# Low-rank product over all 128 rows, adapter products one token tile later, first query chunk two tiles later, in a fused mixing and attention kernel

## The chip, the cores and the metric

The kernel runs on one core of a Trainium2 chip. The metric is the device time of one execution in microseconds (us). Three runs of the kernel before gave 1172.77, 1173.44 and 1174.05 us; the median, 1173.44, is the time before.

The engines are named as in the profile: PE (TensorE, with PEld for its weight loads), DVE (VectorE), ACT (ScalarE), POOL (GpSimd) and SP (SyncE, which here mostly issues DMAs). A matrix product takes its stationary operand through a weight load and streams the other operand's columns. Products land in PSUM, which has eight banks of 2 KB a partition; everything else stands in SBUF, 128 partitions wide.

## The reference

`x` is 32 batches x 32 tokens x 512 features, float32 like everything here. Four layers are added one after the other:

```python
# L0: mix the 32 tokens of a batch with one of 16 small matrices (32 x 32)
x = x + einsum('bct,bcd->bdt', x, weights[condition])
# L1: one base matrix for all, and a low-rank addition with a picked A
low = einsum('bsi,bir->bsr', x, lora_A[labeler_index])        # rank 32, 5 labelers
x = x + einsum('bsi,oi->bso', x, W) + 0.5 * einsum('bsr,or->bso', low, lora_B)
# L2: one of 8 matrices (512 x 512) for each batch
x = x + einsum('bsi,boi->bso', x, weight[adapter_ids])
# L3: attention: 32 query and 8 key heads of 128, rmsnorm and rope on q and k,
#     512 cached keys in 16 pages and 32 new ones a batch, output product Wo
x = x + attention(x, Wq, Wk, Wv, Wo, k_cache, v_cache, ...)
```

## The kernel before

**Tiles and parts.** The 1024 tokens are cut into eight token tiles of 128 (four batches each, `NT` = 8, `BT` = 4), the 512 features into four chunks of 128 (`KC` = 4). The query, key and value matrices form twelve chunks of 512 columns: eight of queries, two of keys, two of values. The program has a first part (L0, L1, L2 and the first query chunk, tile by tile; lines 423 to 667), a second part that projects the other chunks, and a third with the attention. The first ends about 135 us into the span. The change edits only the first part; no instruction of the other two is added or removed.

**One tile's way through the first part.** Each step names its line in the kernel before.

- `gather_mix` (L443): an indirect DMA from GpSimd fetches the mixing matrices `mg` of the tile's four batches.
- `mixers` (L457): VectorE spreads them into a block-diagonal 128 x 128 matrix `md` and adds the identity, so that the product gives x + L0.
- `mix` (L471): four products of 128 columns give the transposed result in PSUM; ScalarE copies it to `x1t` (L475).
- `low_1` (L490): four products with `la`, the A matrices of all five labelers side by side (160 columns). VectorE masks the four that aren't wanted (the pick, L494) and sums what is left to `low`, 128 tokens x 32 (L501).
- `base` (L504 to 516): TensorE transposes `low` (L508, 32 rows come out), ScalarE scales it by 0.5 into `lowt` (L510), four products with the base matrix `wb` fill a PSUM bank (L513), and one product over 32 rows, `lowt` with `lb` (the B matrix), is added to it (L514; the profile counts each float32 product twice, so a "pair"). VectorE copies the bank to `xs` (L516). The sum x + L0 isn't added to it separately: VectorE adds the identity to `wb` once, in four steps (L636).
- `flip_2` (L480, L481): four transposes and ScalarE's copy give `x2t`.
- `adapt` (L533): sixteen products with four batch-picked adapter matrices `wa`, each over a column group of 32; VectorE adds the result to `xs` (L540).
- `transposed(..., "x3t")` (again L480, L481): the transposed input of the projections.
- `projected(c, t, lag)` (L308 to 384): a chunk's four products, then squares on ScalarE (L335), their sums, roots and reciprocals, the rotation on VectorE and GpSimd (L351, L356, L362), four scalings on ScalarE (L366), a transpose on VectorE into `st`, and four DMAs of it to `q_d` from SP (L384). The last two come `lag` projections later than their own.

**What sets the order.** In the loop of the first part, PE's and DVE's instructions stay in the order in which the program writes them (`manual_schedule`). ACT, POOL and SP are placed by a scheduler; `issue_after` keeps an instruction behind another in that placement. Before the loop the order is mix 0, mix 1, low 0, low 1, mix 2, the identity into `wb`, base 0, low 2, flip_2 0, base 1, adapt 0, then `constants` and `angles` (the rotation tables). A round n then takes mix n, base n-1, flip_2 n-2, low n, x3t of tile n-3, adapt n-2, and from n = 4 on the first query chunk of tile n-4. From n = 8 on, where mix and low have run out, that query projection stands ahead of x3t instead of behind the adapter products.

**Buffers.** Eight PSUM banks are in three pools: `ps_tr` (two banks: x1t, low, lowt, x2t, x3t), `ps_m` (four) and `ps_n` (two); `accumulator` takes every third bank from `ps_n` and the others from `ps_m`. `wa` has eight buffers of 1 MB, two tiles' worth, so that the loads for tile t+2 are issued after `adapt(t)` (`adapt_and_load`). `st` has three.

**Loads.** They are all issued by SP, in this order: `la`, held behind the first `mg` by a tiny ScalarE copy into `la` that has to come first (the gate, L581); `wb`, `lb`, the fourth tile of x, the adapter matrices of tile 0, the rotary table `fr`, the norm weights, more of x, the adapter matrices of tile 1, the first query chunk's weights `wq` 0 between tiles 5 and 6 of x, and then the adapter matrices tile by tile with the stores of `st` among them. `wq` 1 stands after round 4's adapter loads.

The functions that the diff touches, and what calls them, with the profile's line numbers:

Of the kernel before, what the change touches and what calls it, by code (L numbers as in the profile page):

```python
# [12 lines left out]
F32 = mybir.dt.float32  # L13
I32 = mybir.dt.int32
AF = mybir.ActivationFunctionType
ALU = mybir.AluOpType
AX = mybir.AxisListType
# [3 lines left out]
P = 128  # L21
B, S, HID = 32, 32, 512
# [5 lines left out]
NT = B * S // P  # L28
BT = P // S
KC = HID // P  # L30
# [27 lines left out]
def cond_resid_kernel(  # L58
# [18 lines left out]
    nc = tc.nc  # L77
# [48 lines left out]
    def constants():  # L126
        with tc.issue_after(rows_known.ins):
            constant_values()
# [163 lines left out]
    def x3t(t: int):  # L292
        return x3_all[:, :, t * P : (t + 1) * P]
# [9 lines left out]
    def load_qkv(c: int, eng=nc.sync):  # L303
        ws[c] = wqps[c % 2].tile([P, KC, HID], F32, tag="wq", name=f"wq_{c}")
        eng.dma_start(out=ws[c], in_=w_qkv[c])
# [85 lines left out]
    def projected(c: int, t: int, lag: int):  # L391
        u = project(c, t)
        if u is not None:
            for stage in (squares, sums, roots, inverses, rotate, scales):
                stage(u)
            ready.append(u)
        if len(ready) > lag or (u is None and ready):
            store_heads(ready.pop(0))
# [22 lines left out]
    with ExitStack() as p1:  # L421
# [3 lines left out]

        wb = w1p.tile([P, KC, HID], F32, name="wb")
        la = w1p.tile([P, KC, NL * R], F32, name="la")
        lb = w1p.tile([R, HID], F32, name="lb")

        ones = w1p.tile([P, HID], F32, name="ones")  # L430
        nc.vector.memset(ones, 1.0)
# [5 lines left out]
        )  # L437

        mgs, x1ts, lows, x2ts, was = {}, {}, {}, {}, {}

        def gather_mix(t: int):
            mg = sp.tile([P, S], F32, tag="mg", name=f"mg_{t}", bufs=4)
# [23 lines left out]
        def mix(t: int):  # L466

            md = mds.pop(t)
            px = ps_tr.tile([P, KC, P], F32, tag="tr", name=f"x1t_ps_{t}")
            for k in range(KC):  # L470
                nc.tensor.matmul(  # L471
                    px[:, k, :], xs[:, t, k * P : (k + 1) * P], md, start=True, stop=True
                )
            x1ts[t] = sp.tile([P, KC, P], F32, tag="x1t", name=f"x1t_{t}", bufs=3)
            nc.scalar.copy(x1ts[t], px)  # L475

        def transposed(t: int, dst: bass.AP, name: str):
            pt = ps_tr.tile([P, KC, P], F32, tag="tr", name=f"{name}_ps_{t}")
            for k in range(KC):
                nc.tensor.transpose(pt[:, k, :], xs[:, t, k * P : (k + 1) * P], ident)  # L480
            nc.scalar.copy(dst, pt)  # L481
# [3 lines left out]
        which = w1p.tile([P, NT, NL], F32, name="which")  # L485

        def low_1(t: int):
            plo = ps_tr.tile([P, NL * R], F32, tag="tr", name=f"low_ps_{t}")
            for k in range(KC):
                nc.tensor.matmul(  # L490
                    plo, x1ts[t][:, k, :], la[:, k, :], start=(k == 0), stop=(k == KC - 1)
                )
            picked = sp.tile([P, NL, R], F32, tag="picked", name=f"picked_{t}", bufs=1)
            nc.vector.tensor_tensor(  # L494
                picked,
                plo.rearrange("p (l r) -> p l r", l=NL),
                which[:, t, :].unsqueeze(2).to_broadcast([P, NL, R]),
                ALU.mult,
            )
            lows[t] = sp.tile([P, R], F32, tag="low", name=f"low_{t}", bufs=3)  # L500
            nc.vector.tensor_reduce(  # L501
                lows[t], picked.rearrange("p l r -> p r l"), AX.X, ALU.add
            )

        def base(t: int):
            xt = x1ts.pop(t)
            plt = ps_tr.tile([R, P], F32, tag="tr", name=f"lowt_ps_{t}")
            nc.tensor.transpose(plt, lows.pop(t), ident)  # L508
            lowt = sp.tile([R, P], F32, tag="lowt", name=f"lowt_{t}")
            nc.scalar.mul(lowt, plt, LORA_SCALING)  # L510
            pb = accumulator(f"base_{t}")
            for k in range(KC):
                nc.tensor.matmul(pb, xt[:, k, :], wb[:, k, :], start=(k == 0), stop=False)  # L513
            nc.tensor.matmul(pb, lowt, lb, start=False, stop=True)  # L514

            nc.vector.tensor_copy(xs[:, t, :], pb)  # L516
# [61 lines left out]
        load_x(1)  # L578
        load_x(2)

        nc.scalar.copy(la[:, 0, 0:1], mgs[0][:, 0:1])  # L581
        gate = nc.sync.dma_start(out=la, in_=lora_a)
        loads = ExitStack()
        loads.enter_context(tc.issue_after(gate.ins))
        nc.sync.dma_start(out=wb, in_=w_base)
        nc.sync.dma_start(out=lb, in_=lora_b)
        load_x(3)
        for b in range(BT):
            load_adapt(b)
# [5 lines left out]
            load_adapt(b)  # L595
        with tc.issue_after(picked[-1]):
            load_x(5)
            load_qkv(0)
            load_x(6)
            load_x(7)  # L600
        with tc.issue_after(rows_known.ins):
# [4 lines left out]
        with tc.manual_schedule(engines={mybir.EngineType.PE, mybir.EngineType.DVE}):  # L606

            idle = ps_tr.tile([P, HID], F32, tag="tr", name="idle_ps")
            for n in (HID, HID, P, P, P, P, P, P):
                nc.tensor.matmul(idle[:, :n], ones[:, :P], ones[:, :n], start=True, stop=True)  # L610

            def ahead_of(t: int):
                if t + 3 < NT:
                    gather_mix(t + 3)
                if t < NT:
                    mixers(t)

            def adapt_and_load(t: int):
                adapt(t)
                if t + 2 < NT:  # L620
                    for j in range(BT):
                        load_adapt((t + 2) * BT + j)


            ahead_of(0)
            mix(0)
            ahead_of(1)
            mix(1)
            ahead_of(2)
            low_1(0)  # L630
            low_1(1)
            mix(2)

            for k in range(KC):
                d = wb[:, k, k * P : (k + 1) * P]
                nc.vector.tensor_tensor(d, d, ident, ALU.add)  # L636
            base(0)
            low_1(2)
            ahead_of(3)
            flip_2(0)  # L640
            base(1)
            adapt_and_load(0)
            constants()
            angles()
            for n in range(3, NT + 3):
                if n < NT:
                    mix(n)
                if n - 1 < NT:
                    base(n - 1)
                if n - 2 < NT:  # L650
                    flip_2(n - 2)
                if n < NT:
                    low_1(n)
                    ahead_of(n + 1)
                if n >= NT and n - 4 < NT:
                    projected(0, n - 4, 1)
                if n - 3 < NT:
                    transposed(n - 3, x3t(n - 3), "x3t")
                if n - 2 < NT:
                    adapt_and_load(n - 2)  # L660
                if 4 <= n < NT:
                    projected(0, n - 4, 1)
                if n == 4:
                    with tc.issue_after(picked[-1]):
                        load_qkv(1)
            projected(1, 0, 2)
            projected(0, NT - 1, 2)

# [430 lines left out]
```

## Time and profile before

| | kernel before |
|---|---|
| median of three runs | 1173.44 us (1172.77 to 1174.05) |
| profiled execution, its own time | 1172.88 us |
| its span, first to last instruction | 1170.9 us |
| PE busy | 1157.9 us (99%) |
| DVE busy | 797.4 us (68%) |
| ACT busy | 752.8 us (64%) |
| POOL busy | 431.4 us (37%) |
| granted TensorE clock | 1.000 |
| moved by DMA | 250.64 MB, 214 GB/s on average |
| PE's share of the chain that ended last | 92% |

The profiled execution took 2.0 us more than its span; that lies around the instructions. Rows of the timeline give the start in us from the span's start, the busy time, the engine, the line, the operation, output and inputs with their tile, the partitions and elements, and how many instructions of one kind stand together; the bracket holds the idle time of the engine ahead of them and what ended it. On PE a row's busy time overlaps the next row's, since products are pipelined: the time that one takes is the distance from its start to the next start. Rows of the stretches give for each window the span, the busy time of PE, PEld, DVE, ACT and POOL, each with its number of instructions, the granted clock, the mean busy share of the 16 DMA engines, and GB/s.

### The profile page before, as it was taken

What the parts mean: (1) busy time and instruction counts of PE and PEld (TensorE: products, weight loads), DVE (VectorE), ACT (ScalarE), POOL (GpSimd) and SP (SyncE); (2) the same over time, 40 slices, a digit from 0 to 9 for tenths busy, and PEclk for the clock granted to TensorE, in tenths of its full rate; (3) what the DMA queues carried; (4) which work ended last, traced back from release to release, by engine and by line L of the source; (5) the groups of instructions that cost most, each with busy time, mean ns of one, the idle gap of its engine ahead of it and who ended that gap; (6) DMA issues with size and microseconds to landing.
All of it is one profiled execution on the core that took longest, in us unless ns stands there. A gap on an engine that the chain in (4) does not pass through costs nothing.

```text
span 1170.9 us, 19713 instructions
## 1 busy us (share of the span) xinstructions
PE 1157.9 (99%) x5512; PEld 745.1 (64%) x5512; DVE 797.4 (68%) x1782; ACT 752.8 (64%) x1652; POOL 431.4 (37%) x567
## 2 busy tenths in 40 slices
PE   8999999999999999999999999999999999999998
PEld 5444444444444467777777777777777777777766
DVE  2433488777777157877777777777777877876861
ACT  1222366565656268877777877877877777877760
POOL 3301444333333044434433443443344344344410
PEclk9999999999999999999999999999999999999999
DMA  8997765655544646789777677767766776775710
GB/s 323 418 355 289 271 188 135 174 159 155 154 113 114 212 132 226 247 269 271 225 242 232 212 223 240 228 210 227 251 208 208 256 226 198 252 247 189 227 45 10
DMA packets 180879, 250.64 MB, mean 214 GB/s; under 512 B 21250, under 2 KB 140674, under 8 KB 175010
## 3 DMA queue, kind: packets, MB, share of 16 engines
q1 hardware_dynamic: 156802, 163.52, 44.8%
q0 software_dynamic: 19216, 69.35, 17.6%
q10 hardware_dynamic: 4752, 16.52, 4.0%
q8 instruction: 45, 0.74, 0.3%
q14 instruction: 64, 0.52, 0.2%
HBM read 219.94 MB, written 29.36 MB: 213 GB/s over the span
## 4 chain that ended last, share of the span: by engine, by line
PE 92%; DMA 2%; DVE 2%; SPq 1%; issue 1%; ACT 1%; POOL 0%; another core or an unknown queue 0%; DVEq 0%; ACTq 0%; POOLq 0%
PE qkv L308 28%; PE o_ps L818 18%; PE f_ps L895 17%; PE s_ps L747 11%; PE s_ps L748 9%; PE adapt L533 2%; PE base L513 2%; PE o_ps L838 2%; DMA wa<-in_w_adapt_dram 1%; PE pn_ps L805 1%; PE f_ps L915 1%; PE f_ps_last L915 1%; SPq L194 1%; PE base L514 1%; DMA kt<-in_k_cache_dram 0%
## 5 line engine op out<-in xcount | busy, mean ns | idle before, releaser
L790 ACT COPY placed<-turned 32x512 f32<-32x512 f32 x539 | 332.1, 616 | 33.0 <-DVE turned L778 23.7
L818 PEld LDWEIGHTS o_ps<-vt,placed 128*128 128x128 f32 x2048 | 267.3, 191 | 117.1 <-issue 95.5
L308 PE MATMUL qkv<-wq,x3t 128*128 128x512 f32 x768 | 336.9, 593 | 0.3 <-ACT vs L315 0.3
L756 DVE CUSTOM_DVE_ANT_0 pr<-s_ps,mask 128x544 f32<-128x544 f32 x256 | 185.4, 724 | 163.0 <-PE s_ps L748 150.5
L765 ACT ACTIVATE pr<-pr,low 128x544 f32<-128x544 f32 x256 | 191.6, 749 | 133.0 <-DVE low L756 91.7
L818 PE MATMUL o_ps<-vt,placed 128*128 128x128 f32 x2048 | 270.5, 275 | 2.2 <-DVE ot L875 1.3
L308 PEld LDWEIGHTS qkv<-wq,x3t 128*128 128x128 f32 x768 | 145.1, 190 | 171.4 <-issue 167.9
L792 POOL COPY placed<-turned 32x512 f32<-32x512 f32 x268 | 163.4, 610 | 230.2 <-DVE turned L778 176.4
L895 PE MATMUL f_ps<-wo,ot 128*128 128x512 f32 x480 | 241.3, 594 | 0.3
L362 POOL TENSOR_TENSOR ra<-ra,rs 128x512 f32<-128x512 f32 x80 | 101.8, 1272 | 220.9 <-DVE rs L356 196.0
L778 DVE STREAM_TRANSPOSE turned<-pr 128x512 f32<-128x512 f32 x256 | 178.6, 697 | 0.1
L747 PE MATMUL s_ps<-kt,qt 128*128 128x288 f32 x512 | 173.6, 421 | 0.6 <-issue 0.4
L748 PE MATMUL s_ps<-kt,qt 128*128 128x256 f32 x512 | 152.4, 379 | 1.5 <-DMA kt<-in_k_cache_dram 1.5
L246 POOL DMA_INDIRECT vt<-in_v_cache_dram,v_idx x128 | 127.8, 998 | 36.0 <-issue 25.0
L366 ACT ACTIVATE ra<-ra,rinv 128x128 f32<-128x128 f32 x320 | 101.8, 390 | 36.2 <-POOL ra L362 21.4
L748 PEld LDWEIGHTS s_ps<-kt,qt 128*128 128x128 f32 x512 | 97.1, 190 | 29.0 <-issue 2.3
L895 PEld LDWEIGHTS f_ps<-wo,ot 128*128 128x128 f32 x480 | 85.8, 190 | 28.2 <-issue 13.9
L794 DVE COPY placed<-turned 32x512 f32<-32x512 f32 x217 | 96.3, 444 | 5.5
L747 PEld LDWEIGHTS s_ps<-kt,qt 128*128 128x128 f32 x512 | 77.4, 191 | 13.3 <-DVE low L756 6.1
L335 ACT ACTIVATE sq<-qkv 128x512 f32<-128x512 f32 x80 | 47.3, 591 | 59.6 <-PE qkv L308 59.0
L801 POOL COPY pq<-pr 128x128 f32<-128x128 f32 x64 | 18.5, 289 | 178.0 <-ACT pr L765 162.2
L351 DVE TENSOR_TENSOR ra<-qkv,cw 128x512 f32<-128x512 f32 x80 | 54.8, 685 | 35.3 <-ACT sq L335 35.3
(97 smaller groups left out, 747.6 us busy)
## 6 DMA issues: line engine op xcount, KB each, us to landing
kt<-in_k_cache_dram SPq DMA_DIRECT2D x512, 128.0 KB
wa<-in_w_adapt_dram SPq DMA_DIRECT2D x32, 1024.0 KB
q_d<-st SPq DMA_DIRECT2D x256, 64.0 KB
qt<-q_d SPq DMA_DIRECT2D x64, 256.0 KB
wq<-in_w_qkv_dram ACTq DMA_DIRECT2D x10, 1024.0 KB
wo<-in_w_o_dram SPq DMA_DIRECT2D x16, 320.0 KB
k_d<-st SPq DMA_DIRECT2D x64, 64.0 KB
v_d<-vs ACTq DMA_DIRECT2D x16, 256.0 KB
```

Source lines behind the costliest of these rows:

```text
L246: nc.gpsimd.indirect_dma_start(out=vts[b][:, c, :], out_offset=None, in_=v_cache, in_offset=bass.IndirectOffsetOnAxis(ap=v_idx[:, at : at ...
L308: nc.tensor.matmul(ps, x3t(t)[:, k, :], ws[c][:, k, :], start=(k == 0), stop=(k == KC - 1))
L362: nc.gpsimd.tensor_tensor(u.a, u.a, s, ALU.add)
L747: nc.tensor.matmul(ps[:, first:L], q, kt4[:, :N_LOW, g, :], start=True, stop=True)
L748: nc.tensor.matmul(ps[:, L : first + LT], q, kt4[:, N_LOW:, g, :], start=True, stop=True)
L756: nc.vector.tensor_tensor_reduce(pr, ps[:, first : first + LT], mask, -SCALE, 3.0e38, ALU.add, ALU.min, low)
L765: nc.scalar.activation(pr, pr, AF.Exp, bias=low, scale=-1.0, accum_out=dens[quad][:, u : u + 1])
L778: nc.vector.transpose(part, pr)
L790: nc.scalar.copy(dst, src)
L792: nc.gpsimd.tensor_copy(dst, src)
L818: nc.tensor.matmul(po, pt[:, c, :], vt[:, c, g * D : (g + 1) * D], start=(c == 0 and q == 0), stop=(c == L // P - 1 and q == 1),)
L895: nc.tensor.matmul(pfs[t][:, :HID], ots[t, h // HALF][:, h % HALF, :], wo(h), start=(h == 0), stop=(h == (HQ if t < NT - 1 else HALF) - 1),)
```

## The change

Three things change in the first part.

The low-rank product runs over 128 rows. `lb` has 128 rows, zeroed by GpSimd and then filled in the first 32; `low` is one of three 128 x 128 tiles that were zeroed once, of which the reduction writes the first 32 columns; its transpose is 128 x 128, stands after the third of the four base products, and the product with `lb` is over all rows. The result of `low_1`'s products takes a bank of `ps_m` and not of `ps_tr`.

The rounds are shifted. Round n has adapt n-3 (was n-2), x3t of tile n-4 (was n-3) and, from n = 6 on, the first query chunk of tile n-6 (was n-4). There is one round more; two of the first chunk's tiles stand behind the loop. `constants` and `angles` follow the first adapter products in round 3.

The loads are moved. `la` goes first without a gate, and the gate is on `wb`. `wq` 0 leaves its place among the first loads for the place behind the fourth tile's adapter matrices, and `wq` 1 goes behind the sixth's. The four additions of the identity to `wb` stand ahead of the first pick on VectorE.

```diff
--- before.py
+++ after.py
@@ -425,7 +425,8 @@
 
         wb = w1p.tile([P, KC, HID], F32, name="wb")
         la = w1p.tile([P, KC, NL * R], F32, name="la")
-        lb = w1p.tile([R, HID], F32, name="lb")
+        lb = w1p.tile([P, HID], F32, name="lb")
+        nc.gpsimd.memset(lb, 0.0)
 
         ones = w1p.tile([P, HID], F32, name="ones")
         nc.vector.memset(ones, 1.0)
@@ -437,6 +438,11 @@
         )
 
         mgs, x1ts, lows, x2ts, was = {}, {}, {}, {}, {}
+
+
+        wide = [w1p.tile([P, P], F32, name=f"low_{i}") for i in range(3)]
+        for low in wide:
+            nc.gpsimd.memset(low, 0.0)
 
         def gather_mix(t: int):
             mg = sp.tile([P, S], F32, tag="mg", name=f"mg_{t}", bufs=4)
@@ -485,7 +491,7 @@
         which = w1p.tile([P, NT, NL], F32, name="which")
 
         def low_1(t: int):
-            plo = ps_tr.tile([P, NL * R], F32, tag="tr", name=f"low_ps_{t}")
+            plo = ps_m.tile([P, HID], F32, tag="mm", name=f"low_ps_{t}")[:, : NL * R]
             for k in range(KC):
                 nc.tensor.matmul(
                     plo, x1ts[t][:, k, :], la[:, k, :], start=(k == 0), stop=(k == KC - 1)
@@ -497,20 +503,21 @@
                 which[:, t, :].unsqueeze(2).to_broadcast([P, NL, R]),
                 ALU.mult,
             )
-            lows[t] = sp.tile([P, R], F32, tag="low", name=f"low_{t}", bufs=3)
+            lows[t] = wide[t % 3]
             nc.vector.tensor_reduce(
-                lows[t], picked.rearrange("p l r -> p r l"), AX.X, ALU.add
+                lows[t][:, :R], picked.rearrange("p l r -> p r l"), AX.X, ALU.add
             )
 
         def base(t: int):
             xt = x1ts.pop(t)
-            plt = ps_tr.tile([R, P], F32, tag="tr", name=f"lowt_ps_{t}")
-            nc.tensor.transpose(plt, lows.pop(t), ident)
-            lowt = sp.tile([R, P], F32, tag="lowt", name=f"lowt_{t}")
-            nc.scalar.mul(lowt, plt, LORA_SCALING)
             pb = accumulator(f"base_{t}")
             for k in range(KC):
                 nc.tensor.matmul(pb, xt[:, k, :], wb[:, k, :], start=(k == 0), stop=False)
+                if k == KC - 2:
+                    plt = ps_tr.tile([P, P], F32, tag="tr", name=f"lowt_ps_{t}")
+                    nc.tensor.transpose(plt, lows.pop(t), ident)
+                    lowt = sp.tile([P, P], F32, tag="lowt", name=f"lowt_{t}")
+                    nc.scalar.mul(lowt, plt, LORA_SCALING)
             nc.tensor.matmul(pb, lowt, lb, start=False, stop=True)
 
             nc.vector.tensor_copy(xs[:, t, :], pb)
@@ -578,12 +585,12 @@
         load_x(1)
         load_x(2)
 
-        nc.scalar.copy(la[:, 0, 0:1], mgs[0][:, 0:1])
-        gate = nc.sync.dma_start(out=la, in_=lora_a)
+        nc.sync.dma_start(out=la, in_=lora_a)
+        nc.scalar.copy(wb[:, 0, 0:1], mgs[0][:, 0:1])
+        gate = nc.sync.dma_start(out=wb, in_=w_base)
         loads = ExitStack()
         loads.enter_context(tc.issue_after(gate.ins))
-        nc.sync.dma_start(out=wb, in_=w_base)
-        nc.sync.dma_start(out=lb, in_=lora_b)
+        nc.sync.dma_start(out=lb[:R, :], in_=lora_b)
         load_x(3)
         for b in range(BT):
             load_adapt(b)
@@ -595,7 +602,6 @@
             load_adapt(b)
         with tc.issue_after(picked[-1]):
             load_x(5)
-            load_qkv(0)
             load_x(6)
             load_x(7)
         with tc.issue_after(rows_known.ins):
@@ -627,22 +633,19 @@
             ahead_of(1)
             mix(1)
             ahead_of(2)
+
+            for k in range(KC):
+                d = wb[:, k, k * P : (k + 1) * P]
+                nc.vector.tensor_tensor(d, d, ident, ALU.add)
             low_1(0)
             low_1(1)
             mix(2)
-
-            for k in range(KC):
-                d = wb[:, k, k * P : (k + 1) * P]
-                nc.vector.tensor_tensor(d, d, ident, ALU.add)
             base(0)
             low_1(2)
             ahead_of(3)
             flip_2(0)
             base(1)
-            adapt_and_load(0)
-            constants()
-            angles()
-            for n in range(3, NT + 3):
+            for n in range(3, NT + 4):
                 if n < NT:
                     mix(n)
                 if n - 1 < NT:
@@ -652,17 +655,21 @@
                 if n < NT:
                     low_1(n)
                     ahead_of(n + 1)
-                if n >= NT and n - 4 < NT:
-                    projected(0, n - 4, 1)
+                if n >= NT:
+                    projected(0, n - 6, 1)
+                if 0 <= n - 4 < NT:
+                    transposed(n - 4, x3t(n - 4), "x3t")
                 if n - 3 < NT:
-                    transposed(n - 3, x3t(n - 3), "x3t")
-                if n - 2 < NT:
-                    adapt_and_load(n - 2)
-                if 4 <= n < NT:
-                    projected(0, n - 4, 1)
-                if n == 4:
+                    adapt_and_load(n - 3)
+                if n == 3:
+                    constants()
+                    angles()
+                if 6 <= n < NT:
+                    projected(0, n - 6, 1)
+                if n in (4, 6):
                     with tc.issue_after(picked[-1]):
-                        load_qkv(1)
+                        load_qkv(n // 2 - 2)
+            projected(0, NT - 2, 1)
             projected(1, 0, 2)
             projected(0, NT - 1, 2)
 
```

## The prediction, on record before the result

> **What bounds the kernel now.** I read the page's busy times and chain first, then TensorE's timeline for the first 135 us (all edits lie there), then the other engines', SyncE's issues and the DMA rate where TensorE waits.
>
> The page:
>
> ```profile
> PE 1157.9 (99%) x5512; PEld 745.1 (64%) x5512; DVE 797.4 (68%) x1782; ACT 752.8 (64%) x1652; POOL 431.4 (37%) x567
> ...
> PE 92%; DMA 2%; DVE 2%; SPq 1%; issue 1%; ACT 1%; POOL 0%; another core or an unknown queue 0%; DVEq 0%; ACTq 0%; POOLq 0%
> ```
>
> TensorE sets the time: whatever shortens its stream in the first part moves the end one for one, since no product of the later parts changes. The start, in the timeline of all engines:
>
> ```profile
> 9.91 1.32 PE L490 MATMUL low_ps<-la,x1t 128*128 128x160 f32 x8 [0.58 <-DMA la<-in_lora_a_dram]
> 11.89 0.59 ACT L475 COPY x1t<-x1t_ps 128x512 f32<-128x512 f32 x1 [2.83 <-PE low_ps L490]
> ...
> 13.77 1.16 PE L471 MATMUL x1t_ps<-md,xs 128*128 128x128 f32 x8
> ...
> 15.32 3.70 PE L513 MATMUL base<-wb,x1t 128*128 128x512 f32 x8 [0.28 <-DVE wb L636]
> ```
>
> The second copy of x1t starts at 11.89 although its products ended at 9.33. TensorE's timeline further on:
>
> ```profile
> 49.21 1.06 PE L533 MATMUL adapt<-wa,x2t 128*32 128x512 f32 x6
> 50.77 3.62 PE L533 MATMUL adapt<-wa,x2t 128*32 128x512 f32 x26 [0.50 <-DMA wa<-in_w_adapt_dram]
> 54.32 3.70 PE L308 MATMUL qkv<-wq,x3t 128*128 128x512 f32 x8
> ...
> 63.94 1.25 PE L490 MATMUL low_ps<-la,x1t 128*128 128x160 f32 x8
> 65.79 0.66 PE L480 MATMUL x3t_ps<-ident,xs 128*128 128x128 f32 x4 [0.60 <-ACT x2t L481]
> ...
> 74.38 0.27 PE L508 MATMUL lowt_ps<-ident,low 128*32 128x128 f32 x1
> 74.49 3.60 PE L513 MATMUL base<-wb,x1t 128*128 128x512 f32 x8
> 78.02 1.12 PE L514 MATMUL base<-lb,lowt 32*128 32x512 f32 x2
> 79.07 0.66 PE L480 MATMUL x2t_ps<-ident,xs 128*128 128x128 f32 x4
> 79.56 1.25 PE L490 MATMUL low_ps<-la,x1t 128*128 128x160 f32 x8
> ```
>
> Read start to start. The third adapter product takes 54.32-49.21 = 5.11 us, the others 3.57: it waits for its weights. Low to x3t takes 1.85, elsewhere 1.09: ScalarE is late. And the 32-row pair (L514) costs more than its columns: 1.05 where a quarter of eight products' 3.44 (qkv 108.27 to 111.71) is 0.86; the base before it takes 3.53, not 3.44; the x2t behind it 0.49, not 4 x 0.11. SyncE's issues, and the DMA stretches behind the last of them:
>
> ```profile
> 84.83 3.08 SPq L158 DMA_DIRECT2D wa<-in_w_adapt_dram  x4
> 92.29 1.75 SPq L384 DMA_DIRECT2D q_d<-st  x4
> 99.63 3.06 SPq L158 DMA_DIRECT2D wa<-in_w_adapt_dram  x4
> ```
>
> ```profile
> 110.00:112.00 2.00, 2.00 (x8) 0.99 (x7) 0.00 (x0) 0.03 (x1) 0.00 (x0) 1.00 0.92 338
> 112.00:114.00 2.00, 2.00 (x22) 0.64 (x24) 1.04 (x3) 1.34 (x3) 0.00 (x0) 1.00 0.35 105
> ```
>
> Four adapter matrices issued at 99.63 have moved (4.2 MB, summed over the stretches) between 112 and 113: 12.4 to 13.5 us after the issue. Those of 84.83 take until about 97.
>
> **The change, part by part.**
>
> *Low-rank pair over 128 rows.* The products keep their number and columns; what goes is 0.19 + 0.09 + 0.05 = 0.33 to 0.34 us at each of eight tiles: 2.7 us. The transposed product now stands between the third and fourth base product; it costs 0.11 as before (74.38 to 74.49). Its copy on ScalarE has to end inside what follows it, 0.11 + 0.86 = 0.97: alone it takes 0.27 + 0.26 plus some 0.06 of signals, so it is covered; behind a copy of 0.59 it took until 32.04 from 31.04 and would cost up to 0.2 a tile. I take 0; bounds 0 and 1.6.
> The Trainium skill (TensorE: Matmul & The Clock Gate, Why this matters for your kernels) says a lone product of 32 rows takes as long as one of 128, by which widening gains nothing and the sum is 2.7 worse. The same skill (TensorEngine Tiling (Array Packing), Key Properties) says that a change of tiling mode drains TensorE. The rows agree with the second at L514, and not at L508, whose 32 columns also change the mode and cost no more than their 0.11; the rows decide.
>
> *Adapter products one tile later.* Tile 2's weights: with the earlier starts below, adapt(0) ends at about 35.4, and the weights issued then land by 49, where adapt(2) is due at 53.7. The wait goes: 1.5 us. wq(0) is issued behind the fourth tile's weights (adapt(1) ends 46.4; 13 us for them, 2.5 for 1 MB at 415 GB/s: 62) and is due at 68; wq(1) has 50 us.
> The low product has banks of another pool now, and x2t a whole round before its use: the 0.8 us at 65.79 goes. The table load (1.28) falls under base(6), before its low-rank copy.
>
> *The tail.* Between adapt(5)'s end and adapt(7) there stood 20.7 us (99.62 to 120.34). Now there stand x2t, qkv, x3t, adapt(6), qkv, x3t: 0.49 + 3.44 + 0.53 + 3.57 + 3.54 + 0.53 = 12.1. Their weights can be issued only at adapt(5)'s end, and on SyncE's queue they now stand behind the second query tile's four stores, which come 3.8 us behind their product (88.45 to 92.29), so just before adapt(5)'s end, and take 1.75: the loads start 1.6 to 1.9 later than that end. 1.7 + 12.4 to 13.5 = 14.1 to 15.2, against 12.1: a new wait of 2.0 to 3.1, up to 3.4 if the stores' small rows share the engines. I take 2.9: the run of 99.63 is the nearest.
>
> *The start.* la (0.33 MB) leaves the gate; wb goes at 6.74 and not 7.14. The identity's four adds (0.89) stand before the first pick on VectorE and wait for wb; even if it lands at 12 they and two picks (1.5) end by 14.5, and the low values are due at 17.2. base(0) follows the third mix directly: 13.77 + 0.89 = 14.66 and not 15.32, if the copy at 11.89 stays late: 0.7 gained. What made that copy late no row shows. Bounds: -0.3 (the gathers share the engines with la; the third, beside it, came about 0.9 slower than the second) and 3.0 (copy at 9.35, base(0) at 12.3). I take 0.7, what these rows show. GpSimd's four memsets (0.55 by the iota of equal width, 3 x 0.2) less the three small jobs that move behind the gathers (0.73) are 0.4, inside its 1.38 idle before the first gather.
>
> *Nothing on the path:* the angles' 7.4 us on VectorE now follow adapt(0) at 35.4; base(3)'s copy, a pick and the next mixer queue behind them and end at 45.4, mix(5) is due at 46.3. If that cover goes, mix(5) pays.
>
> **Sum:** 2.7 + 1.5 + 0.8 + 0.7 - 2.9 = 2.8. The profiled execution took 1172.88 (span 1170.9 and 2.0 around it), so 1170.1; the median shown is 0.56 above it: 1173.44 - 2.8 = **1170.6**, 0.24% less.
>
> **Rivals.**
> *The start clears.* The late copy is gone with la's wait: base(0) at 12.3, 2.3 us more: 1168.3. For it: the copy's releaser is the low product that itself waited for la. Against: low and its pick were late too (ended 11.23, picked 13.39), after la was there. 22%.
> *No wait at adapt(7)*, if the last weights come within 12 us: 1167.7. Against: three batches that took 12.4 or more. 8%.
> *The pair gains nothing*, its copy being late or the drain elsewhere (the first rule above): 1172.5 to 1173.3. Against: equal overheads in every tile's rows. 10%.
> *Slower: the stores.* Four query tiles now run without filler, not three, and in the built order 16 key pages and a 0.4 us load stand before the seventh tile's store, where 13 pages stood. VectorE waited 3.43 us for such a store at 149.9. Pages took 1.4 each, so it comes 4 us later after adapt(7), as the products do by 3.5: a bank that was read at 155.3 and needed at 162 keeps some 6.5 us. Beyond that TensorE pays each us; at 2.2 a page the store is 12 later and the time 1176. 10%.
>
> **How the numbers follow.** My forecast has 50%; its own range is 1169.8 to 1171.8 (new wait 2.0 to 3.4, start -0.3 to 1, copies up to 0.8). 0.2% (2.35 us) is what a measurement of this kernel can tell from no change: below 1171.1 is faster. Two thirds of the forecast (0.33) and the first two rivals (0.30) are faster: 0.63; the rest of it and the third rival are the same: 0.27; slower 0.10. Range 1167.8 to 1172.9: it leaves out the slower rival and the low ends.
>
> **What would show it.** L521 pair to x2t 0.86 at each tile, base with its transposed product 3.55; no wait before adapt(2) to adapt(6); a wait of 2 to 3.4 us on wa before adapt(7) at about 111; base(0) at 14.7; the first product of the second query chunk's second tile near 131.8 (134.7 before). Wrong: if L521 waits for its copy, if adapt(7) does not wait, or if qkv waits for VectorE between 135 and 175.

## The result and the profile after

Over 20 runs each the changed kernel took 1171.84 us and the kernel before 1174.36 (medians); the ratio is 0.9979, 95% interval 0.9972 to 0.9986. That is 2.5 us (1.6 to 3.3) faster, where 2.8 was forecast. The profiled execution's own time is 1172.15 us, its span 1170.3. The page still has TensorE as the bound:

```profile
PE 1155.9 (99%) x5512; PEld 745.8 (64%) x5512; DVE 798.6 (68%) x1782; ACT 753.1 (64%) x1652; POOL 430.7 (37%) x571
...
PE 91%; DMA 3%; DVE 3%; issue 1%; SPq 1%; ACT 1%; POOL 0%; another core or an unknown queue 0%; DVEq 0%; ACTq 0%; POOLq 0%
```

One round of TensorE's timeline, by which the low-rank pair is read:

```profile
72.79 2.74 PE L515 MATMUL base<-wb,x1t 128*128 128x512 f32 x6
75.37 0.27 PE L518 MATMUL lowt_ps<-ident,low 128*128 128x128 f32 x1
75.47 1.02 PE L515 MATMUL base<-wb,x1t 128*128 128x512 f32 x2
76.34 1.02 PE L521 MATMUL base<-lb,lowt 128*128 128x512 f32 x2
77.19 0.60 PE L486 MATMUL x2t_ps<-ident,xs 128*128 128x128 f32 x4
77.63 1.25 PE L496 MATMUL low_ps<-la,x1t 128*128 128x160 f32 x8
78.72 0.60 PE L486 MATMUL x3t_ps<-ident,xs 128*128 128x128 f32 x4
```

The pair now takes 0.85 (76.34 to 77.19; 1.05 before) and x2t behind it 0.44 (0.49). Base with its transposed product takes 3.55 (3.64). The pair does not wait for its copy: 0.87 after the fourth product, as its columns ask. From low to x3t it is 1.09; the 0.76 us that were lost here once are gone. The third adapter set does not wait: its 32 records stand in one row. What came instead stands at the eighth, in the same timeline:

```profile
53.76 3.64 PE L540 MATMUL adapt<-wa,x2t 128*32 128x512 f32 x32
...
110.30 0.60 PE L486 MATMUL x3t_ps<-ident,xs 128*128 128x128 f32 x4
110.83 1.61 PE L540 MATMUL adapt<-wa,x2t 128*32 128x512 f32 x6
114.29 3.62 PE L540 MATMUL adapt<-wa,x2t 128*32 128x512 f32 x26 [1.84 <-DMA wa<-in_w_adapt_dram]
117.84 3.70 PE L308 MATMUL qkv<-wq,x3t 128*128 128x512 f32 x8
```

117.84 - 110.83 less the usual 3.57 is a wait of 3.44 us. SyncE's queue shows why the weights come then:

```profile
98.64 1.76 SPq L384 DMA_DIRECT2D q_d<-st  x4
100.98 3.06 SPq L158 DMA_DIRECT2D wa<-in_w_adapt_dram  x4
```

The sixth adapter set ended at 98.74. The loads that it releases are issued at 100.98, behind the second query tile's stores, and the last products start 13.3 us after that. A second new wait is 0.44 us ahead of the sixth mix: the second adapter set starts at 42.32, so the mix was due at 45.89.

```profile
46.33 1.13 PE L477 MATMUL x1t_ps<-md,xs 128*128 128x128 f32 x8 [0.38 <-issue]
```

The start, in the timeline of all engines:

```profile
2.90 0.43 SPq L588 DMA_DIRECT2D la<-in_lora_a_dram  x1
...
7.91 0.29 DVE L463 TENSOR_TENSOR md<-mg,quarter 128x128 f32<-128x128 f32 x1 [4.10 <-DMA mg<-in_w_mix_dram,c_idx]
...
8.58 2.05 PE L477 MATMUL x1t_ps<-md,xs 128*128 128x128 f32 x16 [1.58 <-DVE md L463]
...
11.18 0.59 ACT L481 COPY x1t<-x1t_ps 128x512 f32<-128x512 f32 x1 [0.81 <-PE x1t_ps L477]
13.01 1.05 PE L477 MATMUL x1t_ps<-md,xs 128*128 128x128 f32 x8
13.59 0.90 DVE L639 TENSOR_TENSOR wb<-wb,ident 128x128 f32<-128x128 f32 x4 [4.01 <-DMA wb<-in_w_base_dram]
13.94 2.84 PE L515 MATMUL base<-wb,x1t 128*128 128x512 f32 x6
```

The first mixer comes at 7.91 (6.60 before), the first mix at 8.58 (7.38 before); yet the first base product starts at 13.94 and not at 15.32. The second copy of x1t, at 11.89 before, is at 11.18 here. The additions to wb wait until 13.59 for wb to land (the prediction allowed for 12), and the first base product follows the first of them by 0.35; it does so in five of the ten profiled runs of the new order, so wb's landing is close to being the next limit there.

At the second query chunk's second tile TensorE is 2.56 us ahead (121.81 + 3 x 3.44 = 132.1 against 134.7). The rows account for 2.46 of it: pair 8 x 0.333 = 2.66, third adapter set 1.54, x2t 0.76, start 1.38, less the two new waits of 3.44 and 0.44.

### The profile page after: what moved, and what is told of

Same layout as the page of the kernel before. It is cut to its first block, busy times and chain, and to the rows that moved or that the text cites. A ratio compares the mean times of both kernels' runs of the same rounds, so it can differ in the third digit from the quotient of the medians.

```text
span 1170.3 us, 19720 instructions
## 1 busy us (share of the span) xinstructions
PE 1155.9 (99%) x5512; PEld 745.8 (64%) x5512; DVE 798.6 (68%) x1782; ACT 753.1 (64%) x1652; POOL 430.7 (37%) x571
## 4 chain that ended last, share of the span: by engine, by line
PE 91%; DMA 3%; DVE 3%; issue 1%; SPq 1%; ACT 1%; POOL 0%; another core or an unknown queue 0%; DVEq 0%; ACTq 0%; POOLq 0%
PE qkv L308 28%; PE o_ps L825 18%; PE f_ps L902 16%; PE s_ps L754 11%; PE s_ps L755 9%; PE base L515 2%; PE adapt L540 2%; PE o_ps L845 2%; DMA kt<-in_k_cache_dram 1%; DMA wa<-in_w_adapt_dram 1%; PE x1t_ps L477 1%; PE pn_ps L812 1%; PE low_ps L496 1%; PE f_ps L922 1%; PE f_ps_last L922 1%
## 6 DMA issues: line engine op xcount, KB each, us to landing
kt<-in_k_cache_dram SPq DMA_DIRECT2D x512, 128.0 KB
```

## The experiments

The kernel before ran beside each group on the same chip. Where an interval stands, it is that of the ratio to it. "Second chunk" is the start of TensorE's product of the second query chunk's second tile, from which on all kernels have the same products; the last column is the span less that. Each row's times are of one profiled run.

| kernel | first mix | first base | wait at the eighth adapter set | second chunk | the rest |
|---|---|---|---|---|---|
| before | 7.38 | 15.32 | 0 | 134.7 | 1036.2 |
| changed | 8.58 | 13.94 | 3.44 | 132.1 | 1038.2 |
| changed, profiled again | 8.17 | 13.24 | 2.59 | 130.6 | 1037.7 |
| pair alone | 7.51 | 13.11 | 0 | 133.3 | 1036.2 |
| narrow pair in the new order | 8.60 | 13.60 | 2.67 | 133.4 | 1035.5 |
| query tile before the last adapter set | 8.14 | 13.25 | 0 | 128.0 | 1035.9 |
| stores behind loads | 7.75 | 12.93 | 0.44 | 128.1 | 1036.9 |
| la gated again | 7.49 | 13.35 | 2.61 | 130.6 | 1037.2 |
| x's third tile behind the gate | 7.50 | 14.02 | 2.74 | 131.4 | 1036.4 |
| pair in halves (order of before) | 7.43 | 15.35 | 0 | 134.9 | 1035.3 |
| mixers before tables | 7.84 | 13.25 | 2.56 | 130.0 | 1037.0 |
| query tile and mixers | 7.79 | 13.21 | 0 | 127.4 | 1037.2 |
| stores and mixers | 7.84 | 13.21 | 0.62 | 128.1 | 1037.6 |

### The pair alone

```diff
 # in the kernel before: lb, low and lowt over 128 rows, zeroed as in the change;
 # the transposed product stays ahead of the base products
-        lb = w1p.tile([R, HID], F32, name="lb")
+        lb = w1p.tile([P, HID], F32, name="lb")
+        nc.gpsimd.memset(lb, 0.0)
...
-            lows[t] = sp.tile([P, R], F32, tag="low", name=f"low_{t}", bufs=3)
+            lows[t] = wide[t % 3]
...
-            plt = ps_tr.tile([R, P], F32, tag="tr", name=f"lowt_ps_{t}")
+            plt = ps_tr.tile([P, P], F32, tag="tr", name=f"lowt_ps_{t}")
```

> Only the low-rank pair over 128 rows, in the order of before (the transposed product still ahead of the base products). My theory (the 32-row pair costs 0.19 + 0.09 + 0.05 us a tile beyond its columns): pair to x2t 0.86 instead of 1.05, x2t 0.44 instead of 0.49, the first tile of the second query chunk's rows 2.6 us earlier than before (132.1 for the second tile, before 134.69), the time 2.5 to 2.8 us under the kernel before. Rival (a lone product takes as long over 32 rows as over 128, and the gain came from the new order): the pair's rows unchanged, the time as before within 0.3 us.

1172.33 us against 1173.62, ratio 0.9992 (0.9984 to 1.0001). Its timeline:

```profile
46.84 2.10 PE L537 MATMUL adapt<-wa,x2t 128*32 128x512 f32 x6
50.38 3.62 PE L537 MATMUL adapt<-wa,x2t 128*32 128x512 f32 x26 [1.44 <-DMA wa<-in_w_adapt_dram]
53.94 3.70 PE L308 MATMUL qkv<-wq,x3t 128*128 128x512 f32 x8
...
65.40 0.66 PE L484 MATMUL x3t_ps<-ident,xs 128*128 128x128 f32 x4 [0.95 <-ACT x2t L485]
...
77.53 1.02 PE L518 MATMUL base<-lb,lowt 128*128 128x512 f32 x2
78.39 0.60 PE L484 MATMUL x2t_ps<-ident,xs 128*128 128x128 f32 x4
78.83 1.25 PE L494 MATMUL low_ps<-la,x1t 128*128 128x160 f32 x8
```

The rows are as the theory has them: 0.86 and 0.44 in the old order too, so the rival falls. The time is not: 2.5 to 2.8 us were expected, the ratio gives 0.9 (-0.1 to 1.9), and TensorE is 1.4 ahead at the second chunk. The third adapter set was due at 46.84 instead of 49.21 and went on at 50.38 instead of 50.77, since its weights came at about the same time. All but 0.4 us of what was gained ahead of it, the start's 2.2 us included, went into that wait, which grew from 1.54 to 3.53; another 0.35 went into the wait ahead of x3t (63.20 to 65.40 is 2.20 from low to x3t, 1.85 before). Why the weights came no earlier: from 10 us to 52 the DMA engines' share is 0.98 to 1.03 in every stretch of this run, so they were full. One of the stretches, share of the engines and GB/s last:

```profile
40.00:45.00 5.00, 5.00 (x18) 2.56 (x18) 0.20 (x2) 0.77 (x2) 5.00 (x5) 1.00 1.03 426
```

So in the old order about half of the pair's 2.7 us (four of the eight tiles stand ahead of that wait) did not reach the end; the shift takes the wait out of the way.

### The narrow pair in the new order

```diff
 # in the changed kernel: lb, low and lowt over 32 rows again
-        lb = w1p.tile([P, HID], F32, name="lb")
-        nc.gpsimd.memset(lb, 0.0)
+        lb = w1p.tile([R, HID], F32, name="lb")
...
-                    plt = ps_tr.tile([P, P], F32, tag="tr", name=f"lowt_ps_{t}")
+                    plt = ps_tr.tile([R, P], F32, tag="tr", name=f"lowt_ps_{t}")
```

> The whole change but with the pair over 32 rows again (transposed product still behind the third base product). My theory: 0.33 us a tile come back, 2.6 in all, less what the wait at the eighth tile's adapter products gives up when TensorE comes later to it: the products up to the sixth adapter set come 6 x 0.33 = 2.0 later and so do the loads that they release, and only the 0.33 between that point and the wait are hidden by it. So 2.3 us slower than the changed kernel, about equal to before (within 0.6 us). Rival: the pair's width is worth nothing and the time stays with the changed kernel, 2.5 under before.

1171.46 us, ratio 0.9989 (0.9979 to 0.9998): 1.3 us under before, where about none was expected. In the trace:

```profile
76.75 0.27 PE L513 MATMUL lowt_ps<-ident,low 128*32 128x128 f32 x1
76.86 1.02 PE L510 MATMUL base<-wb,x1t 128*128 128x512 f32 x2
77.81 1.12 PE L516 MATMUL base<-lb,lowt 32*128 32x512 f32 x2
78.86 0.66 PE L481 MATMUL x2t_ps<-ident,xs 128*128 128x128 f32 x4
79.36 1.25 PE L491 MATMUL low_ps<-la,x1t 128*128 128x160 f32 x8
```

All three parts of the price are back: 0.95 for the product ahead of the pair (0.87 wide), 1.05 for the pair, 0.50 for x2t. Against the changed kernel as profiled again, the second chunk starts 2.9 us later, of which 0.4 is the start; against its first profile 1.3, above all because the wait at the eighth adapter set was 0.8 longer there. By the rows the width is worth 0.33 us a tile in this order too. In the time less can be told: 1.3 us (0.2 to 2.5) under before with the narrow pair, 2.5 (1.6 to 3.3) with the wide one, and the two intervals overlap. The expectation, equal to before within 0.6, missed: it was reckoned from the changed kernel's first profile, whose wait was 0.8 longer than this run's.

### The pair in halves

```diff
-            nc.tensor.matmul(pb, lowt, lb, start=False, stop=True)
+            for h in (0, 1):
+                c = slice(h * HID // 2, (h + 1) * HID // 2)
+                nc.tensor.matmul(pb[:, c], lowt, lb[:, c], start=False, stop=(h == 1))
```

> The kernel before with the 32-row product cut in two halves of 256 columns, still over 32 rows: same columns, one change into and one out of the 32-row form, twice the instructions. If the extra 0.33 us a tile is paid at the change of form: from its first product to x2t still 1.05 to 1.10 us, base before it 3.53, x2t behind it 0.49. If each product over 32 rows pays: 1.25 us or more from its first product to x2t.

```profile
74.73 3.60 PE L513 MATMUL base<-wb,x1t 128*128 128x512 f32 x8
78.26 1.13 PE L516 MATMUL base<-lb,lowt 32*128 32x256 f32 x4
79.31 0.66 PE L480 MATMUL x2t_ps<-ident,xs 128*128 128x128 f32 x4
79.81 1.25 PE L490 MATMUL low_ps<-la,x1t 128*128 128x160 f32 x8
```

One run: 1172.21 us (1173.97 for the kernel before). Twice the instructions over 32 rows, and still 1.05 us from the first to x2t, 3.53 ahead and 0.50 behind. The 0.33 us belong to going into the 32-row form and out of it, not to a product. The Trainium skill (TensorEngine Tiling (Array Packing), Key Properties) says that a change of tiling mode drains TensorE; this trace agrees in so far as the change of rows has a price, 0.33 us for the way in and out; that it is a drain no row shows. There is no such price for the transposed product over 32 columns, which takes 0.11 like the one over 128. The adapter products, though, which have 128 rows and column groups of 32, have longer neighbours in the changed kernel: x3t ahead of them takes 0.53 (110.30 to 110.83) and 0.43 ahead of a query product (121.38 to 121.81), x2t behind them 0.49 (98.74 to 99.23) and 0.44 behind the wide pair. No run here gives them another form, so whether that is the same price is not shown.

### One more query tile ahead of the last adapter set

```diff
-                if n >= NT:
+                if NT <= n < NT + 3:
                     projected(0, n - 6, 1)
+                if n >= NT + 2:
+                    projected(0, n - 5, 1)
...
-            projected(0, NT - 2, 1)
             projected(1, 0, 2)
```

> The change with one more tile of the first query chunk moved ahead of the eighth tile's adapter products (the sixth query tile, whose input is there), and the seventh moved up in the same way; nothing else. My theory: the 3.44 us wait for the last adapter matrices is a matter of the work between the sixth and eighth adapter sets; 3.44 us more work there fills it. Wait 0 to 0.3 us, the second query chunk's second tile at 128.7 to 129.0 (132.1 in the changed kernel), the time 3.1 to 3.5 under the changed kernel and 5.6 to 6.0 under before. Rival: VectorE and the stores cannot follow the query tiles so close together, TensorE waits for PSUM banks behind it, and the time stays with the changed kernel or goes above it.

1167.27 us against 1173.62, ratio 0.9953 (0.9940 to 0.9966): 5.5 us (4.0 to 7.0) under before, 5.6 to 6.0 expected.

```profile
106.08 7.13 PE L308 MATMUL qkv<-wq,x3t 128*128 128x512 f32 x16
113.05 0.60 PE L486 MATMUL x3t_ps<-ident,xs 128*128 128x128 f32 x4
113.58 3.64 PE L540 MATMUL adapt<-wa,x2t 128*32 128x512 f32 x32
117.16 3.70 PE L308 MATMUL qkv<-wq,x3t 128*128 128x512 f32 x8
```

The wait is gone, and the second chunk starts at 128.0, 4.1 us ahead of the changed kernel's first profile (0.7 of it the start) and 2.6 ahead of its second. TensorE's rows show no gap behind it up to 335 us, so it waits for no bank, and the rival falls. The wait was a matter of how much work lay between the sixth set and the eighth.

### The stores behind the loads

```diff
                 if n >= NT:
-                    projected(0, n - 6, 1)
+                    projected(0, n - 6, 2)
```

> The change with the stores of the query tiles lagging by one projection more from the eighth round on, so that the second query tile's four stores stand behind the eighth tile's adapter loads on SyncE's queue and not ahead of them. My theory: the loads are issued at the end of the sixth adapter set (98.8) and not 2.2 us later (100.98), so they land 2.2 earlier: the wait at the eighth adapter set falls from 3.44 to about 1.3 us. Rival (the transfer itself was slowed by what else moved, and the queue place is harmless): the wait stays at 3.0 to 3.5 us.

One run: 1166.94 us (1173.62 for the kernel before).

```profile
97.81 3.04 SPq L158 DMA_DIRECT2D wa<-in_w_adapt_dram  x4
105.68 9.38 SPq L384 DMA_DIRECT2D q_d<-st  x8
```

The loads are issued 0.08 us after the sixth set's end (97.73) and not 2.24 after it; the wait falls to 0.44. Against the 2.6 us that most runs of the new order show, that is 2.1, the queue's share; the expected 1.3 was again reckoned from the one wait of 3.44. The rival falls; the second kernel with these stores, further down, has 0.62.

### la behind the gate again

```diff
-        nc.sync.dma_start(out=la, in_=lora_a)
-        nc.scalar.copy(wb[:, 0, 0:1], mgs[0][:, 0:1])
-        gate = nc.sync.dma_start(out=wb, in_=w_base)
+        nc.scalar.copy(la[:, 0, 0:1], mgs[0][:, 0:1])
+        gate = nc.sync.dma_start(out=la, in_=lora_a)
         loads = ExitStack()
         loads.enter_context(tc.issue_after(gate.ins))
+        nc.sync.dma_start(out=wb, in_=w_base)
```

> The changed kernel with la behind the first gathered matrices again and wb behind la, as before; nothing else. Theory 1 (la's transfer, no longer gated, shares the engines with the first gather, and its landing 1.3 us later is the price): the first mixer comes at 6.1 to 6.6 again, the first mix at 7.4 to 7.5 (8.58 in the changed kernel). For what follows, theory 1a (TensorE's wait for la makes the second copy of x1t late each time): copy near 11.9, base(0) near 14.7. Theory 1b (that lateness is a matter of the single execution, as the pair-alone run without it suggests): lows without a gap, base(0) at 12.9 to 13.1. Rival 2 (the gather's landing has nothing to do with la): first mix at 8.1 to 8.6 still.

One run: 1169.65 us (1173.97 for the kernel before beside this run and the next two). The first mixer comes at 6.51, the first mix at 7.49: the transfer of la beside the gather was what made both late. (It is not the four memsets on GpSimd: the gather is issued between 3.30 and 3.41 in every run.) Low then waits 0.77 us for la (10.21), the second copy of x1t is at 10.49 and not at 11.89, and the first base product at 13.35. So neither 1a nor 1b as put: TensorE's wait for la does not bring the copy's lateness with it each time. Ungated or gated, the first base product comes at the same time within the spread of the runs (12.93 to 13.94 ungated, 13.35 gated). The gain at the start is not la's.

### x's third tile behind the gate

```diff
         load_x(1)
-        load_x(2)
...
+        load_x(2)
         nc.sync.dma_start(out=lb[:R, :], in_=lora_b)
```

> The changed kernel with the third tile of x (0.25 MB) issued behind the gate and not ahead of la, so that the engines have about the bytes of before (two tiles of x and la, not three) beside the first gather. Theory (what is queued ahead delays the gather): first mix at 7.4 to 7.7, base(0) at 12.9 to 13.3 (13.94 in the changed kernel), unless x's third tile, due at 12, becomes the wait. Rival (la alone, whatever its place, delays it): first mix at 8.1 to 8.6.

One run: 1169.65 us. The first mixer comes at 6.82 and the first mix at 7.50. The eight runs with la and all three tiles of x ahead of the gather have the first mixer at 7.05 to 7.93, the four with la behind it at 6.14 to 6.76. So the bytes queued ahead are the likely delay, and not la's place alone; with one run, 0.23 us from the nearest of the eight, that is not more than likely. But the third mix then starts only at 13.06, when the two lows (from 9.39) had long been done, and the first base product at 14.02. x's tile was the one input that had been moved later, so its lateness is the likely cause, as the expectation's clause has it; no row shows it, and the releaser that the trace names is VectorE's addition to wb, which that product does not read.

### The sixth mixer ahead of the tables

```diff
                     low_1(n)
-                    ahead_of(n + 1)
+                    if n != 4:
+                        ahead_of(n + 1)
...
                 if n == 3:
+                    ahead_of(5)
                     constants()
```

> The changed kernel with the sixth tile's mixer (two VectorE instructions) ahead of the rotation tables and not behind them. Theory (the 0.44 us that the sixth mix waits at 45.9 comes from these two instructions, which take 1.19 and 1.25 us beside GpSimd's table products and 0.28 elsewhere): the mixer takes 0.6 us at about 36, the sixth mix follows the second adapter set without a gap (at 3.57 from its start and not 4.01). Rival (another instruction of VectorE or a copy is behind it): a gap of 0.3 us or more stays.

One run: 1168.85 us. First the changed kernel's rows, then this one's:

```profile
43.51 2.57 POOL L580 TENSOR_TENSOR sw<-sn,nw 128x512 f32<-128x512 f32 x2 [21.51 <-ACT sn L566]
43.76 1.19 DVE L463 TENSOR_TENSOR md<-mg,quarter 128x128 f32<-128x128 f32 x1
44.98 1.25 DVE L470 TENSOR_TENSOR md<-md,ident 128x128 f32<-128x128 f32 x1
46.05 1.32 POOL L579 TENSOR_TENSOR sw<-nsn,nw 128x512 f32<-128x512 f32 x1
46.16 0.67 DVE L547 TENSOR_TENSOR xs<-xs,adapt 128x512 f32<-128x512 f32 x1
```

```profile
34.90 0.28 DVE L463 TENSOR_TENSOR md<-mg,quarter 128x128 f32<-128x128 f32 x1
35.22 0.29 DVE L470 TENSOR_TENSOR md<-md,ident 128x128 f32<-128x128 f32 x1
...
41.53 3.64 PE L540 MATMUL adapt<-wa,x2t 128*32 128x512 f32 x32
45.10 1.16 PE L477 MATMUL x1t_ps<-md,xs 128*128 128x128 f32 x8
```

The gap is gone (45.10 - 41.53 = 3.57); it came from these two instructions.

### Both edits together, each way, and the changed kernel again

The first kernel has the extra query tile and the earlier mixer, the second the later stores and the earlier mixer; the third is the changed kernel. Their edits are those shown.

> The changed kernel with both edits that took waits away: one more query tile ahead of the last adapter products, and the sixth mixer ahead of the rotation tables. My theory: the two add, 3.44 + 0.44 = 3.9 us under the changed kernel, 6.4 under before; no wait in TensorE's rows from the first base product to the second query chunk. Rival: the later parts give some of it back (the keys' pages and stores come to SyncE's queue earlier but are not moved faster): 4.5 us or less under before.

> The changed kernel with the query tiles' stores one projection later from the eighth round on, and the sixth mixer ahead of the rotation tables. My theory: the wait for the last adapter matrices is 0.3 to 0.8 us instead of 3.44 (0.44 when the stores alone were moved), the mixer's 0.44 is gone: 3.0 to 3.6 us under the changed kernel, 5.5 to 6.1 under before; 0.3 to 0.8 slower than with the extra query tile. Rival: the single low time of the stores' run was chance and this one stays within 2 us of the changed kernel.

> The changed kernel itself on this chip, beside the two others: 2.0 to 3.0 us under before. Its wait for the last adapter matrices 3.2 to 3.6 us again, the sixth mix 0.4 late again, since both follow from durations and not from the start; the first mix between 7.7 and 8.6, since that differed from run to run.

Against 1173.90 us of the kernel before on that chip: 1168.06, ratio 0.9955 (0.9941 to 0.9968); 1168.87, ratio 0.9957 (0.9943 to 0.9970); and 1170.82, ratio 0.9978 (0.9969 to 0.9987). In its trace the first of them runs without a wait from the first base product to the second chunk, which starts at 127.4, 3.1 us ahead of the changed kernel profiled again: 2.59 + 0.44 = 3.0, so the two edits add. In the time it is 2.7 ahead of that kernel, 5.3 (3.8 to 6.9) under before. That interval holds both the 6.4 expected and the rival's 4.5, so the time doesn't settle whether the later parts give something back, and the 0.44 is too small to be told from the extra query tile alone.

The second has the wait expected (0.62) and starts the second chunk 2.5 us ahead of the changed kernel, but it gains less than the 3.0 to 3.6 expected: 2.0 by the medians, 2.5 by the ratios, whose intervals just overlap. Its rival, under 2 us, is not ruled out by the time. All five of its runs lie above the single 1166.94 us of the later stores alone, so that one time says little.

The changed kernel came 2.6 under before by the ratio, within the 2.0 to 3.0 expected; its sixth mix was 0.44 late again, its first mix at 8.17. But its wait was 2.59 and not the 3.2 to 3.6 expected:

```profile
110.13 1.06 PE L540 MATMUL adapt<-wa,x2t 128*32 128x512 f32 x6
112.74 3.62 PE L540 MATMUL adapt<-wa,x2t 128*32 128x512 f32 x26 [1.55 <-DMA wa<-in_w_adapt_dram]
```

The next products start at 116.29. Of six profiled runs with these loads and this work between, five have 2.56 to 2.74, and the first profile's 3.44 is the exception. The difference lies between issue and landing: the loads were issued 2.24 us after the sixth set's end both times, and the products went on 12.5 us after that here and 13.3 in the first profile.

## Why the prediction came out

*The pair* (2.7 taken, bounds 0 and 1.6 for its copy). Right by its rows, and the copy costs nothing. The halves show that the price is one of changing the form, as the prediction had read it; the rule of the Trainium skill that it weighed against this (TensorE: Matmul & The Clock Gate, Why this matters for your kernels), by which a lone product over 32 rows takes as long as one over 128, doesn't agree with the rows of either order, 1.05 us against 0.86. What the sum does not show is that the term depended on the next one: alone, half of it went into the wait for the third tile's weights.

*Adapter products one tile later* (1.5 and 0.8). Right: no wait at the third set, none at x2t.

*The tail* (2.9, bounds 2.0 and 3.4). Right in cause, and in size but for a hair: 3.44, just beyond the bound, and 2.59 in two profiles. The stores ahead of the loads cost 2.24 where 1.6 to 1.9 was reckoned; from issue to the restart of the products 13.3 and 12.5 were measured, 12.4 to 13.5 reckoned. Work in between and the queue's order each take the wait away.

*The start* (0.7, bounds -0.3 and 3.0). Right within the bounds, wrong in its way. 1.38 and 2.08 us were gained. Two terms stand behind it: the first mix is 1.2 and 0.8 later than before (la's bytes; it had been weighed as at most a loss of 0.3 in all), and a delay of about 2.2 us that the prediction had kept is gone. That delay was in two of the three profiled runs of the old order (base at 15.32 and 15.35) and not in the third (13.11), so the kernel before likely starts now one way, now the other. The prediction laid it on the late copy of x1t, but the copy was late (11.89) in the kernel before alone; in the pair in halves it is at 10.47, and the delay is there. What both have is a late pick of the low product, at 13.39 and 13.42 for products that ended near 11.2, with the third mix right behind it (in the kernel before the second low product, itself behind the late copy, ends there too):

```profile
13.42 0.33 DVE L494 TENSOR_TENSOR picked<-low_ps,which 128x160 f32<-128x160 f32 x1 [4.05 <-PE low_ps L490]
...
13.80 1.16 PE L471 MATMUL x1t_ps<-md,xs 128*128 128x128 f32 x8 [1.33 <-DVE picked L494]
```

These rows are of the pair in halves, where the third mix waits for the pick: low and x1t share the two banks of `ps_tr`. In the changed kernel the pick stands behind wb's additions, at 14.41, after the third mix (13.01), and nothing of the start waits for it: low has a bank of another pool and its transposed product stands behind the third base product. In nine of the ten profiled runs of the new order the third mix waits for nothing on VectorE; the tenth is the one with x's third tile moved. Which of the edits removes the delay was not tried one by one; the rows point to the bank, without showing it. So the rival "the start clears" (22%) named the right outcome in part, for a reason that is not borne out (la's wait; with la gated again TensorE waits for it, and the delay is still gone). What made the pick late in two runs of three stays open.

*Nothing on the path* was wrong for the tables: "end at 45.4, mix(5) is due at 46.3" became 46.23 against 45.89, because the mixer took 2.44 us beside GpSimd's products instead of 0.6. That costs 0.44.

*The slower rival* did not come. VectorE did wait for stores of `st`, 3.45 us at 144.2 and 1.56 at 151.1, but TensorE's rows show no gap from 121.81 to 335.

*The sum.* 2.8 was forecast and 2.5 measured, but that the two are so close is partly luck. The start gave 0.7 to 1.4 more than was taken, the sixth mixer cost 0.44 that was not in the sum, and the last wait was 2.6 or 3.4. TensorE was 2.6 and 4.1 us ahead at the second chunk in two profiles. The rest of the program, with the same products, then differs by up to 2.9 us between profiled runs, from 1035.3 to 1038.2. Up to 1.9 of that lies in one stretch, where TensorE waits for the keys' pages: from the product at 453.0 us in the kernel before to the one at 565.0, the thirteen runs took from 111.0 to 112.9 us. The three runs of the old order average 1035.9 us for the rest, the ten of the new 1037.0. Whether the new order itself gives back that 1 us is not settled.

## What to carry to other kernels

A saving ahead of a wait for a transfer that already fills the DMA engines is lost to that wait: of 2.4 us gained ahead of it with the pair alone, 2.0 went into it. So a row's price is what an edit can save, and the waits behind it say how much of it arrives. When work is shifted towards the end of a stage, count what is left between the point that frees the last buffers and the point that needs their new contents, and look at what stands ahead of those loads in their queue: here 12.1 us of work stood against 14.7 to 15.6 of queueing and loading, and 3.44 us of products moved into the gap were worth about as much again as the whole change. One profile's start or wait is a sample: the wait here was 3.44 us once and about 2.6 five times, and the start of the old order had its delay in two profiles of three.

## What the runs showed of the hardware

- Going into and out of a 32-row product cost 0.33 us in a stream of 128-row products, whether one or two such products (two or four instructions in the profile) stood in between; a transposed product with 32 columns took 0.11 us, as with 128, but the rows ahead of and behind the adapter products, with column groups of 32, were 0.10 and 0.05 longer than beside others.
- Two VectorE products of 128x128 with both inputs in SBUF took 1.19 and 1.25 us beside GpSimd products over SBUF and 0.28 and 0.29 alone; an addition with one input in PSUM, beside another GpSimd product, took 0.67, as usual. The Trainium skill (SBUF — State Buffer, SBUF: two separate sides) says that a VectorE instruction with two SBUF inputs and a GpSimd instruction that reads SBUF lock each other out for a whole instruction; these rows agree, at about the 1.28 us of one GpSimd product a time.
- With 0.33 MB more queued ahead of a small indirect gather, the first instruction that needs it came at 7.05 to 7.93 us (eight runs) and not at 6.14 to 6.76 (four runs); with 0.26 MB of x taken out from ahead of it, at 6.82 (one run).
